# A graph attention layer: rows of constants and of maxima by way of DRAM

## The chip, the cores and the metric

The kernel runs on one core of a Trainium2 chip. The metric is device time of one launch in microseconds (us). Five engines work side by side: TensorE (PE, matrix products, with its weight loads shown as PEld), VectorE (DVE), ScalarE (ACT), GpSimd (POOL) and SyncE (SP, which only issues transfers). Each runs its own list in the order written. ScalarE, SyncE and GpSimd each issue DMAs on a queue of their own, and all queues share 16 DMA engines.

## The reference

Inputs are x (4096 x 512) and a weighted adjacency matrix adj (4096 x 4096), all in float32.

```
q = x Wq' + bq;  k = x Wk' + bk;  v = x Wv' + bv
a = q k' / sqrt(512) + adj + adj
x = layernorm(x + softmax(a) v)                      # layer 0
h = relu(adj (x W1) + b1)
x = layernorm(x + adj (h W2) + b2)                   # layer 1
```

bq, bk and bv are not zero here.

## The kernel before

**Scores.** The kernel folds the two projections into one matrix, M = Wq' Wk (`m_t`), so that a score is x M x' plus terms from the biases. Along the queries one term is left, a number c per query, which needs `g_t` (from Wq and bk) and one constant `c0_t` (bq times bk). The scores are kept transposed: keys lie on partitions, queries along the free dimension. Queries are taken in eight groups of 512 (g = 0 to 7). A number per query is therefore wanted as a row of 512, the same on all 128 partitions.

**Products.** `qk` forms the scores of group g by Strassen's scheme in Winograd's form: seven products of half-size blocks, in the order 1, 2, 6, 7, 5, 4, 3, on one PSUM bank for X and one for Y, which DVE reads after each product (`qk_read`). The softmax of group g - 1 (`shift`, `exps`, `sums`, `px_t2`, `px_t34`, `px_t1`), its product with x (`px_items`) and the closing rows of group g - 2 (`rows_out_fast`, `rows_norm`, `project`, `project2`) are laid between them.

**The order of the work.** It is written out by hand. A group has NP = 16 units, each unit has seven places. `at(unit, place, f)` hangs a piece of work on a place. At each place the loop runs its hooks first, then one product of `qk`, then pieces from a list `todo` that is paid out by a budget in us. s0 is a group's first unit, s1 = s0 + 16 the first unit after its scores, when those of the next group are being formed. Every engine follows the order in which its instructions were issued by this loop.

**A column made into a row.** Two functions turn a column of four numbers per partition into a row of 512 on all partitions. `spread` (L384) multiplies an identity, repeated four times, by the column on DVE: four diagonals side by side, in a slot of the pool `sa`. `in_every_row` (L395) multiplies a matrix of ones with these diagonals on PE into a bank m0 or m1 (`mbank`), and ACT copies the bank out. This is done for bk and bq at the start, for the vector g, and twice in each group:

- c: `add_c0` (L414) adds the constant to the group's four columns and spreads them; `row_consts` (L419) makes the row `cb`. `begin_scores` (L366) copies `cb` on ACT into each block of scores, and `add_scores` (L372) adds adj onto it with an accumulating DMA of GpSimd.
- The maximum: `new_max` keeps a running maximum `macc` on DVE. At place 5 of unit s1 `turn_max` (L461) transposes it on PE, reduces it on DVE to a column m and spreads that; at place 1 of unit s1 + 1 `spread_max` (L467) makes the row `mb`, which every `shift` (L472) subtracts.

**The softmax steps of a pair of key tiles.** A table gives for each of 16 pairs a unit after s1 and three places: the first is the place of the first `shift`, the second that of the second `shift` and of `exps`, the third that of `sums` (the running sum `lacc`, L484/L487) and `px_t2` (L514/L515), both on GpSimd.

```
EARLY, MID, LATE = (1, 2, 4), (2, 4, 6), (3, 5, 6)
PREP = [(1, LATE), (2, EARLY), (2, LATE), (3, MID), ...]
```

Group 0 has `PREP_FIRST`, group 7 `PREP_LAST`, the others `PREP`.

**The closing rows.** `rows_out_fast` (L654, product L698) is paid out from unit s1 + 1 in 14 pieces, for the group before. In its piece (3, 0) it calls `stats(2)` (L668): DVE takes mean and variance of rows 2 and 3 (L673, L674), GpSimd makes the factor and the shift from them (L677 to L681), ACT applies them (`rows_norm`, L634). `project` (L733) transposes the finished rows on PE (x1ps, L735). By the budget the piece (3, 0) falls on place 3 of unit s1 + 2, and the first `project` on place 6.

**The start** (L797 on) loads bk and bq as columns, the weights on SyncE's queue, spreads bk and bq, transposes both weights on PE (psw, L845), multiplies them into M (psm, L854), and has DVE form g, `ub_t` and `c0_t` from the rows (`times`, L826).

Of the kernel before, what the change touches and what calls it, by code (L numbers as in the profile page):

```python
# [11 lines left out]
F32 = mybir.dt.float32  # L12
# [6 lines left out]
P = 128  # L19
W = 512  # L20
# [4 lines left out]
def tile_graph_attention_then_gcn(  # L25
# [51 lines left out]
    nc = tc.nc  # L77
# [3 lines left out]
    ND = D // P  # L81
    NG = N // W
# [3 lines left out]
    PER = W // P  # L86
# [5 lines left out]
    const = ctx.enter_context(tc.tile_pool(name="const", bufs=1))  # L92
    dram = ctx.enter_context(tc.tile_pool(name="dram", bufs=1, space=DRAM))
# [2 lines left out]
    ident = const.tile([P, P], F32, name="ident")  # L96
    ones = const.tile([P, 1], F32, name="ones")
    half_t = const.tile([P, 1], F32, name="half_t")
    bq_t = const.tile([P, ND], F32, name="bq_t")
    bk_t = const.tile([P, ND], F32, name="bk_t")  # L100
    b1_t = const.tile([P, 2], F32, name="b1_t")
    t_sb = const.tile([P, NT, H], F32, name="t_sb")
    c_sb = const.tile([P, NT], F32, name="c_sb")
    c0_t = const.tile([P, 1], F32, name="c0_t")
    ub_t = const.tile([P, ND], F32, name="ub_t")

    u_d = [dram.tile([P, 7, 2, HW], F32, name=f"u_d{g}") for g in range(NG)]
    s_d = {
        (k, d): dram.tile([P, 2, 2, P], F32, name=f"s_d{k}_{d}")
# [41 lines left out]
                6: (S2, T2), 7: (S3, T3)}  # L151
    ORDER = (1, 2, 6, 7, 5, 4, 3)

    FAST_V = range(NG - 2)
    QUARTER = {1: (0, 0), 2: (0, 0), 6: (1, 0), 7: (1, 1), 5: (1, 1), 4: (1, 0), 3: (0, 1)}
    L = {}
    MV, owing = {}, []
    UT, UO, XTS, SA, S, XN, CB, MB, MACC, LACC, O, OT, RL, XR, T = ({} for _ in range(15))
# [225 lines left out]
    def spread(col, name):  # L384

        dg = sap.tile([P, PER, P], F32, tag="sa", name=f"diag{name}")
        nc.vector.tensor_tensor(
            dg,
            ident.unsqueeze(1).to_broadcast([P, PER, P]),
            col.unsqueeze(2).to_broadcast([P, PER, P]),  # L390
            ALU.mult,
        )
        T["diag", name] = dg

    def in_every_row(name, into):  # L395
        dg = T.pop(("diag", name))
        ps = mbank(f"bc{name}")
        nc.tensor.matmul(
            ps, ones.to_broadcast([P, P]), dg.rearrange("p r i -> p (r i)"), start=True, stop=True
        )  # L400
        nc.scalar.copy(into, ps)  # L401
# [12 lines left out]
    def add_c0(g):  # L414
        c = c_sb[:, ts(g, PER)]
        nc.vector.tensor_scalar(c, c, c0_t, None, ALU.add)
        spread(c, f"c{g}")

    def row_consts(g):  # L419
        CB[g] = bcp.tile([P, W], F32, tag="cb", name=f"cb{g}")  # L420
        in_every_row(f"c{g}", CB[g])


    def qk(g, d, k, j):
# [36 lines left out]
    def turn_max(g):  # L461
        ps = turn(MACC[g], f"mt{g}")
        m = small.tile([P, PER], F32, tag="m", name=f"m{g}")
        nc.vector.tensor_reduce(m, ps, AX.X, ALU.max)
        spread(m, f"m{g}")

    def spread_max(g):  # L467
        MB[g] = bcp.tile([P, W], F32, tag="mb", name=f"mb{g}")
        in_every_row(f"m{g}", MB[g])


    def shift(g, q, h):  # L472
# [315 lines left out]
    with tc.tile_pool(name="wqk", bufs=1) as wp:  # L788
        wk_t = wp.tile([P, ND, D], F32, name="wk_t")
        wq_t = wp.tile([P, ND, D], F32, name="wq_t")  # L790
        wk_n = wp.tile([P, ND, D], F32, name="wk_n")
        wq_n = wp.tile([P, ND, D], F32, name="wq_n")
        bq_r = wp.tile([P, W], F32, name="bq_r")
        bk_r = wp.tile([P, W], F32, name="bk_r")
        g_c = wp.tile([P, ND], F32, name="g_c")

        nc.scalar.dma_start(bk_t, bk)  # L797
        nc.scalar.dma_start(bq_t, bq)
        for w_t, wT in ((wq_t, wqT), (wk_t, wkT)):
            for o in range(2):  # L800
                nc.sync.dma_start(
                    w_t[:, :, ts(o, D // 2)],
                    wT.rearrange("(c p) o -> p c o", p=P)[:, :, ts(o, D // 2)],
                )
        make_identity(nc, ident)
        nc.gpsimd.memset(ones, 1.0)
        nc.gpsimd.memset(half_t, -0.5)
        load_xts(0)
        rows0 = t_sb[:, : PER * PER, :].rearrange("p (r a) b -> p r (a b)", r=PER)
        nc.sync.dma_start(rows0, x[:W, :].rearrange("(r p) d -> p r d", p=P))  # L810
        load_xts(1)
        for i in range(4):
            nc.gpsimd.dma_start(
                b1_t[ts(i // 2, H // 2), i % 2 : i % 2 + 1], b1[ts(i % 2, H // 2), :]
            )
        def evict(n, out_, in_):
            if n % 2:
                nc.vector.tensor_copy(out_, in_)
            else:
                nc.scalar.copy(out_, in_)  # L820

        def times(w_t, b_r, into):

            product = t_sb[:, 24 : 24 + PER, :].rearrange("p a b -> p (a b)")
            for c in range(into.shape[1]):
                nc.vector.scalar_tensor_tensor(  # L826
                    product,
                    w_t[:, c, :],
                    HALF_SCALE,
                    b_r,  # L830
                    ALU.mult,
                    ALU.mult,
                    accum_out=into[:, c : c + 1],
                )

        for name, b_t, b_r in (("bk", bk_t, bk_r), ("bq", bq_t, bq_r)):
            spread(b_t, name)
            in_every_row(name, b_r)


        for w_t, w_n in ((wq_t, wq_n), (wk_t, wk_n)):
            for o in range(ND):
                ps = bank("o", f"psw{o}", 4)
                for c in range(ND):
                    nc.tensor.transpose(ps[:, ts(c, P)], w_t[:, c, ts(o, P)], ident)  # L845
                evict(o, w_n[:, o, :], ps)
        times(wq_t, bk_r, g_c)
        spread(g_c, "g")
        times(wk_t, bq_r, ub_t)

        for a in range(ND):
            ps = bank("o", f"psm{a}", 4)
            for o in range(ND):
                nc.tensor.matmul(  # L854
                    ps, wq_n[:, o, ts(a, P)], wk_n[:, o, :], start=o == 0, stop=o == ND - 1
                )
            evict(a, m_t[:, a, :], ps)
            if a == 1:
                in_every_row("g", g_t)
                times(bq_r.unsqueeze(1), bk_r, c0_t)  # L860
                for r in range(PER):
                    row_parts(r, rows0[:, r, :])
                add_c0(0)
# [23 lines left out]
    def at(unit, n, f, *args):  # L887
        n += unit * len(ORDER)
        hooks[n // len(ORDER), n % len(ORDER)].append(lambda: f(*args))
# [157 lines left out]
    def strassen(n, beside, done=()):  # L1047
# [55 lines left out]
    ]  # L1103

    PREP_FIRST = [(1, (2, 3, 4)), (1, (4, 5, 6)), *PREP[2:]]
    PREP_LAST = [
        (1, (2, 2, 3)), (1, (3, 4, 4)), (1, (5, 6, 6)), (2, EARLY), (2, LATE), (3, LATE), (4, MID),
        *PREP[7:],
# [2 lines left out]
    for n in range(NG * NG * len(ORDER)):  # L1111
        (g, d), k = divmod(n // len(ORDER), NG), ORDER[n % len(ORDER)]
        if g:
            unit, place = divmod(2 * (n - 5), len(ORDER))
            at(unit, place, load_s, g, d, k)

    for g in range(NG):
        s0 = g * NP
        s1 = s0 + NP
        if g:  # L1120
            for n, k in enumerate(ORDER):
                at(s0 - 2 + (2 * n + 1) // 7, (2 * n + 1) % 7, load_operand, g, k)
            at(s0 - 2 - (g == 1), 1, add_c0, g)
            at(s0 - 2 - (g == 1), 3, row_consts, g)
        for q in range(NP):
            d, j = divmod(q, 2)
            if (g or d) and j == 0:
                early = 2 + (g == 1 and d < 2)
                at(s0 + q - early, 4, begin_scores, g, d)
                at(s0 + q - early, 5, add_scores, g, d)  # L1130
            for h in range(2):
                n = 1 + 3 * (2 * j + h) if d < NP // 2 - 1 else 2 * j + h
                at(s0 + 2 * d + 2 + n // 7, n % 7, new_max, g, q, h)
            unit, (n0, n1, n2) = {0: PREP_FIRST, NG - 1: PREP_LAST}.get(g, PREP)[q]
            at(s1 + unit, n0, shift, g, q, 0)
            at(s1 + unit, n1, shift, g, q, 1)
            at(s1 + unit, n1, exps, g, q)
            at(s1 + unit, n2, sums, g, q)
            at(s1 + unit, n2, px_t2, g, q)
        at(s1, 5, turn_max, g)  # L1140
        at(s1 + 1, 1, spread_max, g)
        if g < NG - 1:
            at(s1 + 13, 4, row_sums, g)
        at(s1 + 14, 0, load_rows, g)
        at(s1 + 15, 0, add_bv, g)
        px = px_items(g)
        if g == NG - 1:
            for n, (u, k) in enumerate(spare):
                px.insert((8, 14, 20, 26, 90, 150)[n], (0.86, lambda u=u, k=k: product(u, k)))
        if g:  # L1150
            px.reverse()
            by = 3 if g == NG - 1 else 1
            items = row_items(g - 1, lambda n: [px.pop() for _ in range(n * by)])
            work[s1 + 1] = NP, items + px[::-1]
        else:
            work[s1 + 2] = NP - 1, px
# [237 lines left out]
```

## Time and profile before

| | us |
|---|---|
| median of 3 runs | 2328.26 (2327.77 to 2329.89) |
| the profiled execution | 2326.35 |
| its span, first to last instruction | 2324.6 |
| PE busy | 2288.3 |
| DVE, POOL, ACT busy | 1631.5, 1006.0, 403.7 |

The profile is of one execution. A line of a timeline has the start, the duration, the engine, the line of the kernel, the operation, what it writes and reads, and how often it was merged; in brackets stands how long the engine was idle before it, and what ended that. Durations of PE are longer than the distance between its starts, since products overlap. A line with PEclk in the page shows the clock granted to PE; it is full throughout.

### The profile page before, as it was taken

Reading aid. Unit: us, or ns where it says so; the run is one execution under the profiler, and the core shown is the slowest. Engines: PE = TensorE matmul, PEld = TensorE weight load, DVE = VectorE, ACT = ScalarE, POOL = GpSimd, SP = SyncE. Lnnn points to the kernel's source line nnn. Section 1 sums busy time; section 2 is a strip of 40 time slices with the busy share of each in tenths; the row PEclk is TensorE's granted clock in tenths of the full one; section 3 lists DMA queues with packets and bytes.
Section 4 is the critical chain, followed back from the end, with each engine's and each line's share of the span. In section 5 each row is a group of like instructions: output and inputs, shape, how many; then the busy total and the mean of one; then the engine's idle time right before and its main releaser. Section 6 shows DMA issues by size and latency. Waiting matters only on the chain.

```text
span 2324.6 us, 28492 instructions
## 1 busy us (share of the span) xinstructions
PE 2288.3 (98%) x10662; PEld 1752.4 (75%) x10662; DVE 1631.5 (70%) x2295; ACT 403.7 (17%) x445; POOL 1006.0 (43%) x1003
## 2 busy tenths in 40 slices
PE   9998999999999999999999999999999999999998
PEld 5887788888888888888888888888876743333456
DVE  4666776677667766865776686668657867888864
ACT  2212211132112112111311121122102000000012
POOL 2555564175327424741662284236429830001043
PEclk9999999999999999999999999999999999999999
DMA  6998787767857684777577677857664568999996
GB/s 172 275 295 278 228 231 201 208 161 211 221 152 220 187 244 114 218 202 219 145 213 217 163 205 203 223 143 212 187 197 150 166 233 309 333 347 376 344 387 217
DMA packets 277448, 523.30 MB, mean 225 GB/s; under 512 B 19264, under 2 KB 126528, under 8 KB 276416
## 3 DMA queue, kind: packets, MB, share of 16 engines
q1 hardware_dynamic: 229040, 406.12, 52.2%
q0 software_dynamic: 42736, 105.39, 20.6%
q10 hardware_dynamic: 5536, 9.97, 1.2%
q8 instruction: 85, 1.39, 0.2%
q14 instruction: 51, 0.42, 0.0%
HBM read 473.44 MB, written 46.40 MB: 224 GB/s over the span
## 4 chain that ended last, share of the span: by engine, by line
PE 90%; DVE 4%; POOL 3%; issue 1%; DMA 1%; ACT 0%; POOLq 0%; SPq 0%; DVEq 0%; ACTq 0%
PE p L571 31%; PE X L431 17%; PE b L1039 15%; PE Y L431 13%; PE v L698 3%; PE acce L1339 2%; PE psu L224 1%; PE ops L1293 1%; PE tps L744 1%; PE psu L253 1%; PE x L646 1%; POOL uo L214 1%; PE x1ps L735 1%; DVE s L521 1%; DVE s L444 1%
## 5 line engine op out<-in xcount | busy, mean ns | idle before, releaser
L571 PE MATMUL p<-s,xn 128*128 128x256 f32 x3584 | 895.6, 380 | 6.8 <-DVE s L521 3.1
L571 PEld LDWEIGHTS p<-s,xn 128*128 128x128 f32 x3584 | 677.1, 190 | 110.7 <-DVE s L521 6.2
L431 PE MATMUL X<-ut,sa 128*128 128x256 f32 x1984 | 513.3, 381 | 2.2 <-DVE s L444 2.2
L487 POOL TENSOR_TENSOR lacc<-lacc,s 128x512 f32<-128x512 f32 x240 | 344.3, 1435 | 204.1 <-ACT s L478 193.1
L431 PEld LDWEIGHTS X<-ut,sa 128*128 128x128 f32 x1984 | 370.4, 190 | 67.9 <-DVE s L444 15.8
L444 DVE TENSOR_TENSOR s<-X,s 128x512 f32<-128x512 f32 x256 | 176.2, 688 | 281.1 <-PE X L431 280.8
L431 PE MATMUL Y<-ut,sa 128*128 128x256 f32 x1408 | 360.7, 379 | 0.0
L431 PEld LDWEIGHTS Y<-ut,sa 128*128 128x128 f32 x1408 | 266.5, 190 | 39.5 <-issue 4.3
L478 ACT ACTIVATE s<-s 128x1024 f32<-128x1024 f32 x128 | 135.3, 1058 | 790.2 <-DVE s L474 790.2
L453 DVE TENSOR_TENSOR macc<-macc,s 128x512 f32<-128x512 f32 x240 | 255.3, 1064 | 1.2
L375 POOL DMA_DIRECT2D s<-in_adjT_dram x64 | 84.4, 1319 | 366.2 <-ACT s L370 361.5
L444 DVE TENSOR_TENSOR s<-Y,s 128x512 f32<-128x512 f32 x192 | 131.8, 687 | 149.2 <-PE Y L431 148.2
L474 DVE TENSOR_TENSOR s<-s,mb 128x512 f32<-128x512 f32 x256 | 231.0, 912 | 3.3 <-ACT mb L401 3.3
L544 DVE TENSOR_TENSOR ot<-p,ot 128x512 f32<-128x512 f32 x248 | 168.9, 681 | 31.5 <-PE p L571 31.3
L1006 DVE TENSOR_TENSOR tt<-ck 128x1024 f32<-128x1024 f32 x112 | 138.5, 1271 | 40.0 <-PE b L1039 33.7
L1039 PE MATMUL b<-tt,st 128*64 128x512 f32 (+1 forms) x768 | 156.1, 541 | 0.0
L521 DVE TENSOR_TENSOR s<-s 128x512 f32<-128x512 f32 x128 | 130.2, 1038 | 0.0
L514 POOL TENSOR_TENSOR s<-s 128x256 f32<-128x256 f32 x128 | 124.6, 973 | 0.6
L370 ACT COPY s<-cb 128x2048 f32<-128x2048 f32 x64 | 120.9, 1889 | 0.6
L1039 PEld LDWEIGHTS b<-tt,st 128*64 128x64 f32 x768 | 53.9, 137 | 87.8 <-issue 79.9
L515 POOL TENSOR_TENSOR s<-s 128x256 f32<-128x256 f32 x128 | 107.0, 836 | 10.0
L484 POOL TENSOR_TENSOR lacc<-s 128x512 f32<-128x512 f32 x8 | 10.6, 1322 | 201.7 <-ACT s L478 201.7
(189 smaller groups left out, 2125.5 us busy)
## 6 DMA issues: line engine op xcount, KB each, us to landing
ck<-in_adjT_dram SPq DMA_DIRECT2D x128, 1024.0 KB, 7.5
s<-in_adjT_dram POOLq DMA_DIRECT2D x64, 1024.0 KB, 11.1
sa<-s_d SPq DMA_DIRECT2D x224, 256.0 KB, 5.6
xn<-in_x_dram SPq DMA_DIRECT2D x192, 256.0 KB, 3.5
xn<-xs_d SPq DMA_DIRECT2D x96, 512.0 KB, 4.5
sa<-in_xT_dram SPq DMA_DIRECT2D x168, 256.0 KB, 4.6
xn<-xs_d SPq DMA_DIRECT2D x64, 256.0 KB, 3.8
ut<-u_d SPq DMA_DIRECT2D x49, 256.0 KB, 7.4
```

The costliest lines, as they stand in the source:

```text
L431: nc.tensor.matmul(T["X" if k in (1, 6, 5, 3) else "Y"][:, ts(j, HW)], SA[g, d, a][:, c, j, :], UT[g, b][:, c, :], start=k in (1, 2, 7) an ...
L444: nc.vector.tensor_tensor(ck, ps, ck, ALU.add)
L453: nc.vector.tensor_tensor(MACC[g], MACC[g], ck[:, h, :], ALU.max)
L474: nc.vector.tensor_tensor(ck, ck, MB[g], ALU.subtract)
L478: nc.scalar.activation(ck, ck, AF.Exp, scale=2.0)
L487: nc.gpsimd.tensor_tensor(LACC[g], LACC[g], ck[:, h, :], ALU.add)
L514: nc.gpsimd.tensor_tensor(b12, b12, b11, ALU.subtract)
L521: nc.vector.tensor_tensor(b, b, t2, ALU.subtract)
L544: nc.vector.tensor_tensor(to, ps, to, ALU.add)
L571: nc.tensor.matmul(T["PX" if k in (1, 6, 5, 3) else "PY"][:, ts(f, HW)], XN[n][:, q - a, ts(f, P)], quarters(g, q)[{1: 0, 2: 2, 6: 1, 7: 0 ...
L1006: nc.vector.tensor_tensor(t[:, :2], v[:, :, 1], v[:, 0], ALU.subtract)
L1039: nc.tensor.matmul(BK[n][k][ts(half, HH)], lhs, right(u, i, half, b), start=q == 0, stop=q == NP - 1,)
```

## The change

Rows are made by two DMAs in place of a product. `to_row` writes a column of 128 x 4 numbers as a row of 512 to DRAM, `from_row` reads that row onto all 128 partitions. Both are issued by ACT. This is done for bk and bq at the start (there from DRAM to DRAM), for c of groups one to seven, and for the maxima of groups one to six (`ROWS_BY_DMA`). c of group 0, the vector g, and the maxima of groups 0 and 7 stay as they were.

With it the order changes: `add_c0` goes from unit s0 - 2 (s0 - 3 in group 1) to s0 - 4, with the write at place 2 and the read at place 5. The maximum's write is at place 6 of unit s1, its read at place 2 of s1 + 1. In groups one to six the first three pairs of the softmax have new places (`PREP_MID`).

```diff
+    row_d = [dram.tile([1, W], F32, name=f"row_d{n}") for n in range(2 * NG + 2)]
+    ROWS_BY_DMA = range(1, NG - 1)
+    def to_row(n, col):
+        nc.scalar.dma_start(row_d[n].rearrange("o (r p) -> p (o r)", p=P), col)
+
+    def from_row(n, into):
+        nc.scalar.dma_start(into, row_d[n].to_broadcast([P, W]))
...
     def add_c0(g):
         c = c_sb[:, ts(g, PER)]
         nc.vector.tensor_scalar(c, c, c0_t, None, ALU.add)
-        spread(c, f"c{g}")
+        if not g:
+            spread(c, f"c{g}")
 
     def row_consts(g):
         CB[g] = bcp.tile([P, W], F32, tag="cb", name=f"cb{g}")
-        in_every_row(f"c{g}", CB[g])
+        if g:
+            from_row(g, CB[g])
+        else:
+            in_every_row(f"c{g}", CB[g])
...
         nc.vector.tensor_reduce(m, ps, AX.X, ALU.max)
-        spread(m, f"m{g}")
+        if g in ROWS_BY_DMA:
+            T["m", g] = m
+        else:
+            spread(m, f"m{g}")
...
-        in_every_row(f"m{g}", MB[g])
+        if g in ROWS_BY_DMA:
+            from_row(NG + g, MB[g])
+        else:
+            in_every_row(f"m{g}", MB[g])
...
-        nc.scalar.dma_start(bk_t, bk)
-        nc.scalar.dma_start(bq_t, bq)
+        for n, b in enumerate((bk, bq)):
+            nc.scalar.dma_start(row_d[2 * NG + n].rearrange("o (c p) -> p (o c)", p=P), b)
+        for n, b_r in enumerate((bk_r, bq_r)):
+            from_row(2 * NG + n, b_r)
...
-        for name, b_t, b_r in (("bk", bk_t, bk_r), ("bq", bq_t, bq_r)):
-            spread(b_t, name)
-            in_every_row(name, b_r)
...
+    PREP_MID = [(2, (0, 1, 1)), (2, (1, 2, 3)), (2, (4, 6, 6)), *PREP[3:]]
...
-            at(s0 - 2 - (g == 1), 1, add_c0, g)
-            at(s0 - 2 - (g == 1), 3, row_consts, g)
+            at(s0 - 4, 1, add_c0, g)
+            at(s0 - 4, 2, lambda g: to_row(g, c_sb[:, ts(g, PER)]), g)
+            at(s0 - 4, 5, row_consts, g)
...
-            unit, (n0, n1, n2) = {0: PREP_FIRST, NG - 1: PREP_LAST}.get(g, PREP)[q]
+            unit, (n0, n1, n2) = {0: PREP_FIRST, NG - 1: PREP_LAST}.get(g, PREP_MID)[q]
...
         at(s1, 5, turn_max, g)
-        at(s1 + 1, 1, spread_max, g)
+        if g in ROWS_BY_DMA:
+            at(s1, 6, lambda g: to_row(NG + g, T["m", g]), g)
+        at(s1 + 1, 1 + (g in ROWS_BY_DMA), spread_max, g)
```

More of the change, by code (lines that the diff above doesn't have):

```diff
@@ L98, in tile_graph_attention_then_gcn @@
     half_t = const.tile([P, 1], F32, name="half_t")
-    bq_t = const.tile([P, ND], F32, name="bq_t")
-    bk_t = const.tile([P, ND], F32, name="bk_t")
     b1_t = const.tile([P, 2], F32, name="b1_t")
```

## The prediction

> **What bounds the kernel now.** I read the page first, then the waits of PE, then the timelines of five engines around one boundary between query groups (655 to 695 us). Busy totals of the page:
>
> ```profile
> PE 2288.3 (98%) x10662; PEld 1752.4 (75%) x10662; DVE 1631.5 (70%) x2295; ACT 403.7 (17%) x445; POOL 1006.0 (43%) x1003
> q1 hardware_dynamic: 229040, 406.12, 52.2%
> q0 software_dynamic: 42736, 105.39, 20.6%
> ```
>
> PE is idle for only 36 us, and between 665 and 880 us, one whole group, for 0.43 us of 215. What leaves PE's list there leaves the time, unless a new wait takes its place. The PE timeline, with a product of ones with a diagonal and the one wait of the group:
>
> ```profile
> 663.44 1.03 PE L698 MATMUL v<-wv_t,ot 128*128 128x256 f32 x4
> 664.30 1.02 PE L398 MATMUL bcm<-diagm,ones 128*128 128x512 f32 x2
> 665.16 1.03 PE L431 MATMUL X<-ut,sa 128*128 128x256 f32 x4
> ...
> 688.04 1.03 PE L431 MATMUL Y<-ut,sa 128*128 128x256 f32 x4
> 689.44 0.66 PE L735 MATMUL x1ps<-ident,xr 128*128 128x128 f32 x4 [0.37 <-ACT xr L634]
> ```
>
> Starts follow at 0.86 us: that is what one product costs. One place (a seventh of a unit) is two such steps, 1.73 us. The wait at 689.44 is for a normalised row. It comes by DVE statistics (L674), four small GpSimd operations (L677 to L681) and ScalarE (L634). GpSimd, then DVE, then ScalarE, in the same stretch:
>
> ```profile
> 674.74 1.26 POOL L484 TENSOR_TENSOR lacc<-s 128x512 f32<-128x512 f32 x1 [32.57 <-ACT s L478]
> 686.60 0.55 POOL L677 TENSOR_TENSOR rstd<-mv,rl 128x2 f32<-128x2 f32 x1 [8.99 <-DVE mv L674]
> 688.31 0.22 POOL L681 TENSOR_SCALAR shift<-shift 128x2 f32<-128x2 f32 x1
> 688.51 2.62 POOL L487 TENSOR_TENSOR lacc<-lacc,s 128x512 f32<-128x512 f32 x2
> 691.08 1.18 POOL L514 TENSOR_TENSOR s<-s 128x256 f32<-128x256 f32 x1
> 692.34 0.72 POOL L515 TENSOR_TENSOR s<-s 128x256 f32<-128x256 f32 x1
> ...
> 659.62 0.69 DVE L387 TENSOR_TENSOR diagm<-ident,m 128x512 f32<-128x512 f32 x1
> 669.42 0.68 DVE L474 TENSOR_TENSOR s<-s,mb 128x512 f32<-128x512 f32 x1
> 677.19 0.97 DVE L474 TENSOR_TENSOR s<-s,mb 128x512 f32<-128x512 f32 x1
> 681.24 1.28 DVE L474 TENSOR_TENSOR s<-s,mb 128x512 f32<-128x512 f32 x2
> 686.34 0.18 DVE L674 BATCH_NORM_AGGREGATE mv<-stats 128x2 f32<-128x6 f32 x1
> ...
> 681.96 1.06 ACT L478 ACTIVATE s<-s 128x1024 f32<-128x1024 f32 x1 [7.31 <-DVE s L474]
> 688.57 1.52 ACT L634 ACTIVATE xr<-xr,shift,rstd 128x512 f32<-128x512 f32 x2 [0.39 <-POOL shift L681]
> ```
>
> The statistics' GpSimd work (686.60) stands ahead of the sums of the second pair (688.51), although that pair's exponentials were done at 683.02: the list puts it so.
>
> **The Trainium skill.** "DMA: Bandwidth & Descriptors", Rules for kernel authors: a strided last dimension becomes one descriptor per element, and a DMA that reads what another wrote must wait for its semaphore. So a row is 512 pieces of 4 bytes, and the read holds ScalarE's queue until they land. No run so far shows such a DMA. "TensorE: Matmul & The Clock Gate", Architectural detail: ACT and DVE are strict first-in first-out, GpSimd per core. The trace agrees: L487 sat 5.5 us behind L677. "SBUF — State Buffer", Two separate sides: DVE with two SBUF inputs and GpSimd hold their shared port exclusively for a whole instruction. The trace agrees: L474 takes 0.68 us alone and 0.97 beside L515.
>
> **Products removed.** Seven c and six maxima: 13 x 0.86 = 11.2 us of PE, none hidden by other work. With each go a DVE multiply of 0.69 and an ACT copy of 0.59; both engines idle between such pieces (DVE 1.74 us before L464, ACT 24.97 before its copy), so I count nothing; were PE waiting for them, 13 x 1.28 = 17 us more would go, and it isn't. They also held `sa` slots that SyncE's loads of operands wait for; no PE wait is for `sa`. Two bank turns fewer per group leave the fast row products behind the read of L464, done long before.
>
> **Start.** The two products end at 9.01. Without them the transposes of wq can start when it lands (0.73 + 4 to 5.2 us), but those of wk wait for its second half, about 2.26 + 7.9 = 10.2. Eight more transposes at 0.12 us put the first psm product near 11.3 instead of 13.2: at best 1.9 us. Against it stands ACT, which sits behind two row writes before its first eviction. The rows must be in SBUF by about 14.5, since bcg needs g_c at 18.2 and 3.6 us of DVE work lie between. Issue at 0.72, a landing of 3.3 (bk_t) to 7.7 (bq_t's 5.0 and the 2.7 below), a second issue, a read of 3.5 to 8.9: 7.5 to 18. I take 1.2 us of gain (ends: 1.9, and a loss of 1).
>
> **A row's round trip.** Write: from the 3.3 us of bk_t up to 3.3 + 32 pieces per engine (512 over 16) x packet time. A packet takes 52.2% x 16 x 2324.6 / 229,040 = 85 ns on q1 and 179 ns on q0. Alone that adds 2.7 us. With one packet of each other queue between pieces it adds 32 x 349 ns = 11.2. Read, 256 KB: 3.5 us (xn's median) to 8.9 (bv_t, also broadcast). Together 6.8 to 23; I take 11 (3.3 + 2.7 + 5), since little else moves there (28% DMA share at 663 to 676). The maximum of this group is ready at 660.3 (L464 starts at 658.89). The first shift, now at place 0 of the second unit, reaches DVE at 676.3; less two issues of 0.5 that leaves 15. So it is hidden, with 4 us to spare. What ACT holds back meanwhile is nothing: between 665.95 and 673.59 it idled. For c the cover is longer: c_sb is complete and its row first needed 13 places (22 us) later. The c write stands on ACT ahead of the last block's begin_scores, on which GpSimd's accumulating DMA waits; that block is read 11 places (19 us) on, and copy and DMA take 1.9 + 11.1, so 6 us cover a write that waits only for a 0.23 us addition on DVE. The c read stands behind it. SyncE issues none of the new DMAs. In group one, ACT also evicts u products (L206), and PE waits for those about 2.5 us after they fall due; I allow 0.3 us. Each row's 256 KB is small against 523 MB.
>
> **The moved first three pairs.** The first pair's shifts go from places 3 and 5 of unit one to 0 and 1 of unit two. The second pair's sums go from place 4 to place 3. The statistics of rows 2 and 3 are issued at place 3, after the hooks of that place: GpSimd's order turns round, and the sums and px_t2 of the second pair stand ahead of L677. All PE times are 0.86 earlier by then:
> - DVE: L444 674.9, L666, three shifts and the first maximum to 678.8, L444 679.2, L666, then the second pair's last shift at 680.4.
> - GpSimd, first pair: exponentials 677.7 to 678.7, sums to 680.1, px_t2 to about 681.6 plus what the port costs. That last shift meets L514/L515 on the port, so it ends at 681.0 to 681.5.
> - Second pair: exponential to 682.1 to 682.6, then 2.62 + 0.8 + 0.8 = 4.2 us, or 4.9 if the third pair's shift gets in: GpSimd is free at 686.4 to 687.5.
> - L677 could have started at 686.60 - 0.86 = 685.7. It is 0.7 to 1.8 later and PE's wait grows by as much; I take 1.45, since both port meetings look likely.
>
> Six groups (one to six all use the fast row products): 6 x 1.45 = 8.7 us come back, 4.5 to 11. Each group removes two products, 1.72, and returns 1.45. The last group's maximum and its first shifts stay.
>
> **Sum.** -11.2 - 1.2 + 8.7 + 0.3 = -3.4 against the profiled execution (2326.35, with 2324.6 of span and 1.75 around it): 2323.0. The median of the runs lies 1.91 above that execution: **2324.9 us**. Own range of this case: 2321 to 2328. A measurement can tell about 0.2%, 4.7 us, from no change.
>
> **Rivals.**
> - **PE keeps all of it** (26%): the wait at x1ps doesn't grow, because port or semaphore order lets L677 in earlier. For: such waits total only 3.1 us now. Against: program order and strict queues. -11.2 - 1.2 + 0.3: 2316.2.
> - **The row comes late, slower** (19%): beyond 15 us for both landings the first shift holds DVE, with L666 and L444 behind it, GpSimd's sums slip too, and PE waits at x1ps about one for one in six groups. At 17 us it costs 6 x 2 = 12 and gives 2337; at 15.6 it breaks even with before. For: 4-byte pieces, never seen here. Against: the upper bound needs busy queues throughout.
> - A third, ACT held at the start until after 11 us, costs the start's 1.9 and perhaps one more; it lies inside the first case.
>
> **Chances.** Likeliest 55%: 13 points of it, with a wait grown by less than 1.2, lie below 2323.6, the rest within. All-kept: 25 of 26 faster. Late row: 13 slower, 6 within. Faster 0.38, same 0.49, slower 0.13. The range reaches into the gaining case to 2317 (about 7 points beyond) and into the late one to 2333 (about 11 beyond).
>
> **What would show it.** No L398 for c1 to c7 and m1 to m6; group period down from 215.7 (bcm to bcm, 664.30 to 879.98) by 0 to 1, not 1.7; x1ps waiting about 1.8 us per group, on L634, with L487 of the second pair ahead of L677; no DVE wait on mb; psm starting near 11.5. Wrong if x1ps still waits 0.4 (then 2316), or if L474 waits on a DMA.

## The result and the profile after

The changed kernel takes 2339.81 us (median of 6 runs, 2338.41 to 2342.33); the kernel before, beside it, 2326.89 (2325.04 to 2329.89). The ratio is 1.0057, with a 95% interval of 1.0044 to 1.0070: slower by 13 us. The prediction, 2324.9 with a range to 2333, pointed the other way.

The profiled execution of the changed kernel has a span of 2340.5, against 2324.6. It took 2342.28 and so lies near the top of its six, while the one before, 2326.35, lies near its median: the two traces differ by 15.9 us, 3 more than the medians. Of the page after, the busy totals and two queues (packets, MB, share of the 16 DMA engines' time; q10 is ScalarE's):

```profile
PE 2283.4 (98%) x10632; PEld 1753.2 (75%) x10632; DVE 1595.0 (68%) x2280; ACT 392.7 (17%) x430; POOL 1005.7 (43%) x1003
q1 hardware_dynamic: 229040, 406.12, 52.4%
q10 hardware_dynamic: 15328, 13.93, 2.0%
```

PE lost only 4.9 us of its busy time, not 11.2, although the products are gone. ACT lost 11.0, and DVE 36.5, more than its 15 multiplies of 0.69 explain. In the view of PE's waits three kinds stand out (total us, times, longest):

```profile
PE psu L224 <- ACT uo L206: 11.3, 4, 5.1
PE psw L860 <- DMA wq_t<-in_wqT_dram: 10.1, 2, 8.3
PE x1ps L752 <- ACT xr L651: 7.6, 6, 1.3
PE psw L860 <- DMA wk_t<-in_wkT_dram: 4.5, 1, 4.5
```

Here psu is a bank of u, the products of x with M, which ScalarE (L206) copies out to `uo` and GpSimd stores; psw and x1ps are banks of transposes. Before, psu waited 3.4 and x1ps 3.1; at the start PE waited 4.9 for the diagonal of bk. Landmarks of both PE timelines place the loss: the first score product (L431, now L442), and the transposes of the first and of the last group's maximum (L458, now L469).

| stretch | before | after | difference |
|---|---|---|---|
| start, to the first score product | 42.40 | 52.73 | +10.3 |
| scores of group 0, to its maximum | 202.11 | 215.05 | +12.9 |
| seven groups, to the last maximum | 1487.23 | 1480.71 | -6.5 |
| the rest | 592.86 | 592.01 | -0.9 |

**Where the groups repeat, the change does what the prediction said.** The same boundary as before, PE first, then GpSimd, DVE and ScalarE (all times are 21.6 later than before):

```profile
708.78 1.03 PE L442 MATMUL Y<-ut,sa 128*128 128x256 f32 x4
711.06 0.66 PE L752 MATMUL x1ps<-ident,xr 128*128 128x128 f32 x4 [1.26 <-ACT xr L651]
...
704.17 2.63 POOL L504 TENSOR_TENSOR lacc<-lacc,s 128x512 f32<-128x512 f32 x2 [0.58 <-ACT s L495]
706.76 0.73 POOL L531 TENSOR_TENSOR s<-s 128x256 f32<-128x256 f32 x1
707.57 1.06 POOL L532 TENSOR_TENSOR s<-s 128x256 f32<-128x256 f32 x1
708.59 0.19 POOL L694 TENSOR_TENSOR rstd<-mv,rl 128x2 f32<-128x2 f32 x1
...
697.93 1.89 DVE L491 TENSOR_TENSOR s<-s,mb 128x512 f32<-128x512 f32 x3
...
681.21 0.40 ACTq L397 DMA_DIRECT2D row_d<-m  x1
692.29 0.33 ACTq L400 DMA_DIRECT2D mb<-row_d  x1
710.20 1.52 ACT L651 ACTIVATE xr<-xr,shift,rstd 128x512 f32<-128x512 f32 x2 [4.32 <-POOL shift L698]
```

No product of ones is left here. The second pair's sums (L504 to L532) now stand ahead of the statistics (L694), and PE waits 1.26 at x1ps where it waited 0.37. The row of the maximum was written in 11.1 and read in 3.7; DVE's first shift (697.93) shows no wait for it.

**At the start the weights are late.** Of the changed kernel, the DMA issues (us from issue to landing), then SyncE's third load:

```profile
wq_t<-in_wqT_dram SPq DMA_DIRECT2D x2, 512.0 KB, 9.1
wk_t<-in_wkT_dram SPq DMA_DIRECT2D x2, 512.0 KB, 17.0
row_d<-in_bk_dram ACTq DMA_DIRECT2D x1, 2.0 KB, 10.5
row_d<-in_bq_dram ACTq DMA_DIRECT2D x1, 2.0 KB, 16.1
...
11.28 0.37 SPq L163 DMA_DIRECT2D xt<-in_xT_dram  x1
```

Before, the weights landed in 4.6 and 7.4, and this load was issued at 2.85. Between 6 and 8 us from the start the core moves 23 GB/s, where it moved 273. SyncE's queue, which carries the weights, in these two us, after and then before (packets, MB, share of the 16 engines' time):

```profile
q1 hardware_dynamic: 44, 0.05, 98.6%
...
q1 hardware_dynamic: 545, 0.55, 88.7%
```

The DMA engines are not idle there. Their time goes to packets of the weights themselves, 44 where this queue had 545, and no packet of the rows is on record in this stretch. The psm products begin at 22.49, not at 13.21.

**In group 0 a store is late.** ScalarE's and PE's timelines around the write of c of group one:

```profile
198.79 0.38 ACTq L397 DMA_DIRECT2D row_d<-c_sb  x1
214.90 0.84 ACT L206 ACTIVATE uo<-psu,ub_t 128x256 f32<-128x256 f32 x2 [13.79 <-DMA u_d<-uo]
218.76 0.84 ACT L206 ACTIVATE uo<-psu,ub_t 128x256 f32<-128x256 f32 x2 [3.02 <-DMA row_d<-c_sb]
...
215.79 2.08 PE L224 MATMUL psu<-sa,t_sb 128*128 128x256 f32 x4 [5.14 <-ACT uo L206]
217.66 1.78 PE L442 MATMUL Y<-ut,sa 128*128 128x256 f32 x4
219.28 1.03 PE L224 MATMUL psu<-sa,t_sb 128*128 128x256 f32 x4
```

GpSimd's store of `uo`, issued at 195.90, took 18.9 us to land; the one at this place before took 10.2. ScalarE's eviction at 214.90 waits for it, the one at 218.76 for c's row, whose read stands ahead of it, and PE waits 5.14 for a bank. Then PE runs at half pace: 2.08 and 1.78 in place of 1.03, at a granted clock of 0.51 over 3.5 us; after the 4.04 us wait of the next block it is 0.50 over 5.5. The Trainium skill, "TensorE: Matmul & The Clock Gate", What's actually happening, says so: after about 3.4 us idle PE runs at half clock until it has been busy about as long. The trace goes further: PE also ran at about half clock for some 3.4 us each after waits of 1.88 us (from 154.3) and 2.10 us (from 198.7), and in the kernel before after one of 2.09 (from 184.7), which the profile's PEclk row, full throughout, doesn't show. So a wait of 3.4 us isn't needed for it: the measurement decides. Of the 12.9 us, longer waits at psu are 7.9 (11.3 - 3.4). PE worked at half clock for about 16 us in place of 3.4, and half of that difference is 6.3. A product fewer (0.86) and shorter waits for DVE at X (5.6 in place of 6.3) take a little off.

### The profile page after: what moved, and what is told of

Read it like the earlier page. It is cut to its first block, busy times and chain, and to the rows that moved or that the text cites. A ratio compares the mean times of both kernels' runs of the same rounds, so it can differ in the third digit from the quotient of the medians.

```text
span 2340.5 us, 28409 instructions
## 1 busy us (share of the span) xinstructions
PE 2283.4 (98%) x10632; PEld 1753.2 (75%) x10632; DVE 1595.0 (68%) x2280; ACT 392.7 (17%) x430; POOL 1005.7 (43%) x1003
## 4 chain that ended last, share of the span: by engine, by line
PE 87%; POOL 5%; DMA 3%; DVE 3%; issue 2%; ACT 1%; ACTq 0%; POOLq 0%; SPq 0%; DVEq 0%
PE p L588 31%; PE X L442 17%; PE b L1054 14%; PE Y L442 12%; PE acce L1358 2%; PE v L715 2%; DMA u_d<-uo 2%; PE psu L224 1%; PE ops L1312 1%; PE tps L761 1%; PE psu L253 1%; POOL lacc L504 1%; PE x L663 1%; POOL s L532 1%; DMA row_d<-in_bq_dram 1%
## 5 line engine op out<-in xcount | busy, mean ns | idle before, releaser
L442 PE MATMUL X<-ut,sa 128*128 128x256 f32 x1984 | 514.9, 382 | 2.2 <-DVE s L455 2.2
L504 POOL TENSOR_TENSOR lacc<-lacc,s 128x512 f32<-128x512 f32 x240 | 342.1, 1425 | 236.1 <-ACT s L495 225.2
L442 PEld LDWEIGHTS X<-ut,sa 128*128 128x128 f32 x1984 | 371.5, 190 | 65.9 <-DVE s L455 15.8
L442 PE MATMUL Y<-ut,sa 128*128 128x256 f32 x1408 | 361.8, 380 | 0.0
L442 PEld LDWEIGHTS Y<-ut,sa 128*128 128x128 f32 x1408 | 267.5, 191 | 37.4 <-issue 1.4
L464 DVE TENSOR_TENSOR macc<-macc,s 128x512 f32<-128x512 f32 x240 | 246.0, 1025 | 1.2
L532 POOL TENSOR_TENSOR s<-s 128x256 f32<-128x256 f32 x128 | 110.9, 866 | 10.0
L538 DVE TENSOR_TENSOR s<-s 128x512 f32<-128x512 f32 x128 | 102.3, 820 | 0.0
## 6 DMA issues: line engine op xcount, KB each, us to landing
s<-in_adjT_dram POOLq DMA_DIRECT2D x64, 1024.0 KB, 11.7
```

What stands on the lines that cost most here:

```text
L442: nc.tensor.matmul(T["X" if k in (1, 6, 5, 3) else "Y"][:, ts(j, HW)], SA[g, d, a][:, c, j, :], UT[g, b][:, c, :], start=k in (1, 2, 7) an ...
L464: nc.vector.tensor_tensor(MACC[g], MACC[g], ck[:, h, :], ALU.max)
L504: nc.gpsimd.tensor_tensor(LACC[g], LACC[g], ck[:, h, :], ALU.add)
L532: nc.gpsimd.tensor_tensor(b12, b22, b12, ALU.subtract)
```

## The experiments

Theory A: 4-byte writes to DRAM hold up other transfers that are under way or issued beside them. Rival B: the writes are harmless, and what costs is the row's own lateness and ScalarE standing at its read. Rival C: the new order costs, in every group.

**The start back to products.**

```diff
-        for n, b in enumerate((bk, bq)): ...      # the writes
-        for n, b_r in enumerate((bk_r, bq_r)): ...  # the reads, from_row
+        nc.scalar.dma_start(bk_t, bk)
+        nc.scalar.dma_start(bq_t, bq)
...
+        for name, b_t, b_r in (("bk", bk_t, bk_r), ("bq", bq_t, bq_r)):
+            spread(b_t, name)
+            in_every_row(name, b_r)
```

> The changed kernel with bk and bq alone made by products again. Theory of the pieces (writes in 4-byte pieces occupy the DMA engines, hold up SyncE's queue and delay the weights): the first psm product returns from 22.5 to about 13.2, and the time falls by what the start lost, 9.3 to 10.3 us, to about 2329.5. Rival (PE starts cold and late but the later stages would have waited anyway): less than 4 us of it comes back, 2336 or more.

Measured: 2324.98, ratio to before 0.9998 (0.9989 to 1.0007). The psm products start at 12.69 and the weights land in 4.6 and 7.7. This one edit of the start gives 14.8 us, more than the 10.3 of the start itself: group 0's scores also take 207.8 in place of 215.1. That the start is the reason for this second part is not shown; the last experiment speaks against it.

**The start with reads alone**, bk and bq lying as rows in the input.

```diff
-        for n, b in enumerate((bk, bq)): ...
-        for n, b_r in enumerate((bk_r, bq_r)): ...
+        nc.scalar.dma_start(bk_r, bk.to_broadcast([P, W]))
+        nc.scalar.dma_start(bq_r, bq.to_broadcast([P, W]))
...
```

> The changed kernel with bk and bq given as rows in the input, so that the same two 256 KB broadcast reads stay and only the two writes in 4-byte pieces go. Theory of the pieces: no loss at the start, psm starts at 11 to 12.5, 2327.5 to 2328.5. Rival (the broadcast reads of one DRAM row, on ScalarE's queue, are what disturbs the weights): as the changed kernel, 2338 to 2341.

Measured: 2330.05, ratio 1.0018 (1.0008 to 1.0028). psm starts at 15.68, and the weights land in 7.6 and 10.7. Without the writes psm is 6.8 us earlier (22.49 - 15.68), though still 2.5 later than before (runs with products at the start have 11.7 to 13.2): two 256 KB reads issued beside the weights have a price of their own. In the changed kernel the reads come behind the writes.

**As the first, and c of group one by a product at its old place.**

```diff
-        if not g:
+        if g < 2:
             spread(c, f"c{g}")
...
-        if g:
+        if g > 1:
             from_row(g, CB[g])
...
+            at(s0 - (3 if g == 1 else 4), 1, add_c0, g)
+            if g > 1:
+                at(s0 - 4, 2, lambda g: to_row(g, c_sb[:, ts(g, PER)]), g)
+            at(s0 - (3 if g == 1 else 4), 3 if g == 1 else 5, row_consts, g)
```

> As the kernel with the start by products, and also c of group one by a product at its old place. Theory of the pieces: the store of u that took 18.9 us beside the row write takes 10 to 11 again, and the first stage gives back 6 to 9 us: 2321 to 2323. Rival (the first stage lost its time because the late start shifted PE against the stores of u): already back with the start, no more than 2 us below the kernel with the start by products.

Measured: 2317.89, ratio 0.9971 (0.9962 to 0.9980), 7.1 us less than the first. The store of `uo` lands in 11.0 again and psu waits 3.1 in all. One product of 0.86 more on PE saves 7 us.

**As that, and the second pair's sums back at place 4.**

```diff
-    PREP_MID = [(2, (0, 1, 1)), (2, (1, 2, 3)), ...]
+    PREP_MID = [(2, (0, 1, 1)), (2, (1, 2, 4)), ...]
```

> As the last, and the second pair's sums back at place 4 in groups one to six, so that the statistics stand ahead of them on GpSimd. Theory of the turned order: the wait before the transposes x1ps falls from about 1.2 to at most 0.4 us in each of six groups, 4 to 5 us: 2316.5 to 2318. Rival (the wait comes from the first pair's later exponentials or from the shared port): within 1 us of the kernel before it in this call.

Measured: 2315.80, ratio 0.9957 (0.9943 to 0.9972), faster than both kernels. The wait in question, in its view of PE's waits:

```profile
PE x1ps L754 <- ACT xr L653: 3.1, 7, 0.9
```

That is the value of before. Rival C is right for this wait, and for no more than 4 to 5 us. The seven groups take 1476.6, against 1481.0 in the run with the sums at place 3. The two medians lie only 2.1 apart, since group 0's scores vary by 2 to 4 us between executions (201.2 to 205.1 over all kernels without c's row there). The clock goes with this spread: where PE had two stretches of about 3.4 us at half clock in group 0, they took 203.9 to 205.1, and with one or none 201.2 to 202.1. So the wait is settled by the trace rather than by the median.

**A write that nobody reads, beside the store of `uo`, in the kernel before.**

```diff
+    row_e = dram.tile([1, W], F32, name="row_e")
...
+            if g == 1:
+                at(s0 - 4, 2, lambda: nc.scalar.dma_start(row_e.rearrange("o (r p) -> p (o r)", p=P), ub_t))
```

> The kernel before, with one write of 512 pieces of 4 bytes added on ScalarE at the place at which the changed kernel writes c of group one (nobody reads it; c of group one stays a product). Theory, the pieces themselves hold up the store of u next to them: the store takes 15 us or more to land in place of about 11, ScalarE's L206 waits for it, the psu products wait about 3 us more in all, and the time is 4 to 7 us above before, about 2331. Rival, what costs is ScalarE standing at the read behind the write: there is no read here, so the time stays within 1.5 us of before and the store lands in about 11.

Measured: 2330.56, ratio 1.0016 (1.0009 to 1.0022), some 4 us more. The write takes 18.3 to land, the store 14.1. So the write costs without any reader. The size of the waits was missed, though: psu waits 3.8 in all against 3.4, and the profiled execution shows only 1.8 of the 4 us in group 0's scores (203.9 against 202.1), within their spread. There PE has one half-clock stretch more than before, as runs without any such write have too. This execution (2326.62) is one of the fastest of 20. That the write costs time rests on the medians, and how it reached PE isn't shown by this trace.

**The same 2 KB as 128 pieces of 16 bytes.**

```diff
+    row_e = dram.tile([P, PER], F32, name="row_e")
...
+            if g == 1:
+                at(s0 - 4, 2, lambda: nc.scalar.dma_start(row_e, ub_t))
```

> The same 2 KB written at the same place, but each partition's four numbers stay together: 128 pieces of 16 bytes. If the cost goes by the piece, the write lands in well under half of the time that 512 pieces take, the store of u in at most 12.5 us, and the time is 0 to 2 us above before. If it goes by the issue or the bytes, it is like the write of 512 pieces.

Measured: 2325.43, ratio 0.9995 (0.9986 to 1.0004). The write lands in 9.0, the store in 10.8. Bytes, issue and place are those of the run above, so the form of the pieces is the cause there. Since c's row as a whole costs about 8 (7.1 and the product's 0.86) and the write alone 4 to 5, the rest probably falls to ScalarE standing at the read (3.0 and 4.4 us in group 0). That part was not run alone.

**Only c of groups two to seven as rows.**

```diff
-    ROWS_BY_DMA = range(1, NG - 1)
+    ROWS_BY_DMA = ()
-    PREP_MID = [(2, (0, 1, 1)), ...]
+    PREP_MID = PREP
```

with the start and c of group one as in the third experiment.

> Only c of groups two to seven by way of DRAM; bk, bq, c of group one and all maxima stay products, and the softmax steps keep their places of before. Six products fewer on PE: 6 x 0.86 = 5.2 us less than before, about 2320.7, with the x1ps waits at 0.37 to 0.39 as before and the row of c unnoticed by PE. If the write of c costs PE as much in every group as in the first, six groups give back 6 x 4 us and it is above before.

Measured: 2320.03, ratio 0.9975 (0.9965 to 0.9984). From one group's maximum to the next, the six stretches up to group 6's are 0.81 to 0.85 shorter each: a removed product is worth its 0.86, and c's rows cost nothing where they fall in the later groups.

**The rows of bk and bq read on SyncE's queue behind the weights**, otherwise as with the sums at place 4.

```diff
+        nc.sync.dma_start(bk_r, bk.to_broadcast([P, W]))
+        nc.sync.dma_start(bq_r, bq.to_broadcast([P, W]))
```

> As with the sums back at place 4 and c of group one by a product, but bk and bq lie as rows in the input and are read onto all partitions on SyncE's queue behind the two weights. Theory, what hurts at the start is what goes ahead of or beside the weights: here the weights land in about 5 and 8 us as before, psm starts at 11.5 to 13, and the time is 0 to 2 us below that of products at the start, 2314 to 2316. Rival, the rows are late themselves: bcg and ub_t wait for them and the first score product starts later than 42 us, which gives 2318 or more.

Measured: 2315.84, ratio 0.9952 (0.9936 to 0.9968). The weights land in 4.2 and 8.4, psm starts at 12.86: nothing gained over the products at the start and nothing lost.

**Four writes of different sizes in places meant as quiet, groups two to four of the kernel before.**

```diff
...
+    def as_row(t, n):
+        nc.scalar.dma_start(t.rearrange("o (r p) -> p (o r)", p=P), ub_t[:, :n])
...
+    for g in (2, 3, 4):
+        for n, f in enumerate((
+            lambda: as_row(e512, 4),
+            lambda: as_row(h256, 2),
+            lambda: as_row(q128, 1),
+            lambda: nc.scalar.dma_start(k128, ub_t),
+        )):
+            at(g * NP + 4 + 2 * n, 0, f)
```

> The kernel before, with four writes added on ScalarE in each of groups two to four, in places away from the start and from the store of u, which nobody reads: 512, 256 and 128 pieces of 4 bytes, and 128 pieces of 16 bytes. If a write costs a fixed time plus so much for each piece, the landing times fall in line: about 9.7 us for 512 as with the maxima, about 6.5 for 256 and about 5 for 128, and 128 pieces of 16 bytes take the same as 128 of 4. If the fixed part is nearly all, all four land in 8 to 10 us. PE's waits do not change in either case, and the time stays within 2 us of before.

Measured, in one execution of each: 2348.10 beside 2323.53. Both expectations fell. Landing took 9.2, 10.7, 9.5 and 5.5, not in line with the number of pieces, and each of the three groups became 6 to 7 us longer. The places weren't quiet: the 256 pieces at unit 6 were issued 0.4 us behind the second of GpSimd's four stores of `xb` in the group. These landed later (median 7.4 against 4.6). SyncE issued no load between 512.84 and 526.62 (before: 510.63 to 517.43): by the profile a load of `sa` stood 13.3 us for such a store, against 6.4 at the longest before, and the loads of `xn` stand behind it in SyncE's list. PE waited up to 3.9 for `xn`. So the loss came to PE by way of another queue's list. The 512 pieces at unit 4, with no such store near, held up nothing that can be seen: PE's starts fall behind those of before from 523.8 us on, not earlier.

**One place, four sizes**: one write in each of groups two to five at unit 6, place 0.

```diff
+    at(2 * NP + 6, 0, lambda: as_row(e512, 4))
+    at(3 * NP + 6, 0, lambda: as_row(h256, 2))
+    at(4 * NP + 6, 0, lambda: as_row(q128, 1))
+    at(5 * NP + 6, 0, lambda: nc.scalar.dma_start(k128, ub_t))
```

> The kernel before, with one write on ScalarE at the same place (unit 6, place 0) of groups two, three, four and five: 512, 256 and 128 pieces of 4 bytes, then 128 pieces of 16 bytes. It is the place at which 256 pieces made PE wait 3.8 us and the group 7 us longer. Theory, pieces of 4 bytes hold up the store of xb that GpSimd issues 0.4 us ahead: the groups with 512 and 256 pieces are 6 us or more longer than their 214.8 and 215.7 us of before, the one with 128 about 2, the one with 128 pieces of 16 bytes within 0.5. Rival, any write at this place does it: all four groups are 6 to 7 us longer.

Measured, in one execution of each: 2341.55 beside 2327.51. The groups are longer by 5.2, 5.5, 4.4 and -0.5 us. The DMA issues of this run, in the order of the four writes:

```profile
e<-ub_t ACTq DMA_DIRECT2D x1, 2.0 KB, 10.5
h<-ub_t ACTq DMA_DIRECT2D x1, 1.0 KB, 11.0
q<-ub_t ACTq DMA_DIRECT2D x1, 0.5 KB, 10.8
k<-ub_t ACTq DMA_DIRECT2D x1, 2.0 KB, 5.1
```

128 pieces of 4 bytes cost nearly what 512 do, and 128 of 16 bytes cost nothing. It isn't the count, as the expectation had it, and not the place alone, as its rival had it: it is the form of 4-byte pieces. (Pieces of 4 bytes also lie closer together in DRAM, 128 of them in 512 bytes in place of 32. No run separates that from their size.)

The trace also shows where the time isn't. The 512 packets of 4 bytes took 9 ns each at the median, as those of 16 bytes did, and all stood on record by 517.1, 4.1 us after the issue. The row landed at 523.5. With 16 bytes the last packet is on record 4.2 us after the issue, and the landing follows 0.9 later. What goes on in the 6 us between, the trace doesn't show.

**One size, four distances** from the stores of `xb`, 512 pieces each.

```diff
+    for g, unit, place in ((2, 5, 3), (3, 5, 5), (4, 6, 2), (5, 6, 5)):
+        at(g * NP + unit, place, lambda: as_row(e512, 4))
```

> The kernel before, with the same write of 512 pieces of 4 bytes in groups two to five, at four distances from the first of GpSimd's stores of xb: about 7 us and 3.5 us ahead of it, and 3.5 us and 8.7 us after it. Theory, what counts is a store issued while the pieces are under way: the write 7 us ahead costs its group under 2 us, the ones 3.5 us ahead and 3.5 us after cost 4 to 8 us, the last one under 2. Rival, the pieces cost the same wherever they are: all four groups are about 7 us longer.

Measured, in one execution of each: 2335.89 beside 2327.51. The distances came out other than meant: 3.7 us ahead of the second of the four stores, 0.4 and 0.5 behind it, and 7.3 behind the last. The groups are longer by 4.1, 5.1, 3.2 and 0.0. A write near the stores costs, one behind them all doesn't.

**The changed kernel, with bk and bq written in the order in which they lie.** The numbers of the two rows come back in another order, so the bias terms are other numbers; the waits and issues are the same. The expectation counts 128 pieces of 16 bytes; in the trace each of the two writes is 16 packets of 128 bytes. So this run takes the 4-byte pieces away, and doesn't test pieces of 16.

```diff
-            nc.scalar.dma_start(row_d[2 * NG + n].rearrange("o (c p) -> p (o c)", p=P), b)
+            nc.scalar.dma_start(row_d[2 * NG + n].rearrange("o (p c) -> p (o c)", p=P), b)
```

> The changed kernel with bk and bq written to DRAM as they lie, 128 pieces of 16 bytes each in place of 512 of 4; the rows that come back then hold the numbers in another order, so the bias terms are other numbers. All waits and issues are those of the changed kernel. Theory, the number of pieces holds the weights and SyncE's list up: the weights land in 5 to 6 and 8 to 11 us, SyncE issues its third load before 6 us, the psm products start near 15.5 us, and the time is 6 to 8 us below that of the changed kernel. Rival, what costs is the round trip with its two reads behind the writes: psm stays near 22.

Measured, in one execution: 2328.82, some 11 us below the changed kernel's median. Its DMA issues at the start:

```profile
wq_t<-in_wqT_dram SPq DMA_DIRECT2D x2, 512.0 KB, 4.3
wk_t<-in_wkT_dram SPq DMA_DIRECT2D x2, 512.0 KB, 6.7
row_d<-in_bk_dram ACTq DMA_DIRECT2D x1, 2.0 KB, 4.0
row_d<-in_bq_dram ACTq DMA_DIRECT2D x1, 2.0 KB, 4.8
```

psm starts at 10.77, 11.7 us earlier than in the changed kernel and 0.9 to 2.4 earlier than with products. The round trip and both reads are still there, so all of the start's loss goes with the 4-byte pieces. The reads, issued at 4.77 and 6.21 while wk was still on its way, cost nothing that shows here.

Group 0's scores take 214.2 in this run, with c's row landing in 19.7 and the store of `uo` in 19.3, although they begin at 39.96, earlier than before. So a late start isn't needed for that loss.

## Why the prediction was wrong

- **Products removed, -11.2: right.** With c alone, six groups each gave 0.81 to 0.85. The six maxima gave 5.6 more over the seven groups (1482.2 with c alone, 1476.6 with the sums at place 4).
- **The turned order, +8.7: right in kind, too large.** The wait at x1ps grew by 0.89 in each of six groups, 5.3 us, and went back with place 4. (One wait of 0.86 elsewhere fell away, so the total grew by 4.5.) The statistics on GpSimd start 1.25 later relative to PE (708.59 - 21.6 against 686.60 - 0.86), as worked out; but L694 took 0.19 where L677 took 0.55, and that 0.36 was not in the sum.
- **The row of the maximum, hidden: right, with its size off.** The trip took 14.3 to 15.1 in the six groups, not 11. It stayed hidden because the cover was longer than the 15 taken: 16.7 us from the write's issue at 681.21 to the shift at 697.93. The rival of a late row came near the time with a mechanism that no trace shows: no DVE wait on `mb` from DRAM.
- **The start, -1.2: the step that failed; it measured +10.3.** It asked when the two rows would be ready and when ScalarE would be free. It took a landing of 3.3 to 7.7 (measured: 10.5 and 16.1) and left the weights' landing as it was, 10.2 for the second half of wk. The writes moved that to about 19 (2.26 + 17.0). The step's arithmetic of the transposes holds when the weights are in time: without 4-byte pieces the start gained 2.4 on before in one execution (last experiment), though other executions with products there lie up to 1.5 below before's 42.40.
- **c of group one, +0.3: the other step that failed; it measured about 8 (7.1 and the product's 0.86).** It named ScalarE's evictions of u as what PE waits for, but priced only ScalarE's own standing there. The store of `uo` that those evictions wait for, on another queue, was not asked after. Group 0's scores took 12.9 longer in the profiled execution. With c's row there, four executions took 207.8, 210.6, 214.2 and 215.1, and without it they fall to 201.2 to 205.1. What decides between 208 and 215 is open; it isn't the start, which was early in the run with 214.2.
- Behind both stands one sentence of the prediction: a packet's time from queues of large packets, times 32 pieces, added to a landing. That prices what the write needs and not what it does to others, and the price itself was of another kind: the row was 512 packets as counted, but they took 9 ns each, not 85. Those of the maximum written at 681.21 were all on record by 684.6, and the row landed at 692.3. The upper bound for a write, 3.3 + 11.2 = 14.5, was passed at the start (16.1) and in group 0 (19.5).

## What to carry to other kernels

Before a small transfer is added, list the transfers under way and those issued until it lands (9 to 20 us here), and ask who waits for them; the new one's own deadline is the smaller question. A row made of 4-byte pieces belongs where no weight load or store with a reader close behind is in flight; pieces of 16 bytes avoided the problem here, and so did rows already laid out, when they were read behind the weights. And a PE wait of 4 to 5 us, at times one of 2, is paid in part a second time, at half clock.

## What the runs showed that was not expected

- Writing 4-byte pieces to DRAM took 8.4 to 19.7 us to land, over all runs, about the same for 128 pieces as for 512. At the same places 128 pieces of 16 bytes took 5.1 against 10.5 to 11.0, and 9.0 against 18.3. While such a write was under way beside the stores of `xb`, the core's DMA fell to 0 to 25 GB/s for some 6 us, although PE went on to wait for loads. The Trainium skill, "DMA: Bandwidth & Descriptors", has two sentences that bear on it: its Specifications say that below 512 B a read-modify-write is done, and Back-pressure in remote DMA, on transfers between cores, says that stalled writes stall an engine's other queues too. The second fits the 44 packets of weights that took 98.6% of the engines' time at the start, though these transfers stay on one core. The first alone can't be the reason, since 16 bytes lie below 512 as well and cost nothing here; why 4 differ from 16 stays open.
- SyncE's load of `xt`, the first behind the weights, needs neither row. It was issued at 11.28, just as bk's row had landed, and in the last experiment at 4.77, again as that row had landed. By the profile SyncE waited for that row (8.4 us). Before the change, too, its loads of `sa` wait for stores of `xb`. What ties these transfers together was not settled.
